# Layer 1 of a four-layer model: the choice of experts a block ahead of scan and experts' rows, in place of scan, choice and rows one block behind another

## The chip, the core and the metric

The kernel runs as one program on one core of a Trainium2 chip. The metric is device time in microseconds (us) of one execution. Most executions agree within 0.3%. The engines are named as in the profile: PE (matrix multiply; PEld is its weight load), DVE (vector), ACT (scalar), POOL (GpSimd), SP (queue of plain DMAs).

## The reference, cut to what matters

Four layers follow each other over x of shape (2, 2048, 256), that is 4096 tokens of 256 values. Each layer normalizes x and adds an attention-like branch and a feed-forward branch of the same normalized values. The change is in layer 1 alone:

```python
xn = _layernorm(x)
x = x + L1_attn(xn) + L1_ffn(xn)

def L1_attn(x):                      # the "scan" branch
    h = layernorm(x) * g + b
    xs, gate = split(h @ W_in)       # 512 + 512
    xs = silu(causal_conv4(xs) + conv_b)
    delta = mean(softplus(xs @ Wd + bd))
    y = selective_scan(xs, delta)    # 16 states, in order along each sequence
    return x + (y * silu(gate)) @ W_out

def L1_ffn(x):                       # the "choice of experts" and the "rows" branch
    sim = product keys: 8 heads x 2 halves x 128 keys
    sx, ix = top_k(sim[0], 16);  sy, iy = top_k(sim[1], 16)
    scores, index = best of all sums sx + sy           # one expert of 4096 per head
    gate = relu(scores)
    hidden = x @ W_in.T
    hidden += sum over heads of (x . in_a[index]) * gate * in_b[index]
    hidden = gelu(hidden)
    return hidden @ W_out.T + sum over heads of (hidden . out_a[index]) * gate * out_b[index]
```

As one expert per head is kept, the best pair is the best key of each half: the kernel takes two maxima and their places.

## The kernel before, in words

Everything is float32. All of x stays on the chip (`g.x`, 128 partitions x 32 tiles x 256). Layer 0 ends with results of its own experts in a DRAM table (`yd`); layer 1 gathers them into x as it starts (`fetch_experts`, lines 162 to 170: per tile of 128 tokens two indirect DMAs on POOL's queue into `yg`, each followed by a DVE multiply-add, line 169).

Layer 1 handles the tokens in 16 blocks of 256 (2 tiles of 128). Work on a block comes from three Python generators, each cut into steps by `yield`:

- `scan_block`, 9 steps. Step 1 gathers layer 0's results for the block after this one, normalizes the block (`norm2`, lines 737 to 752, into `xn`) and transposes it (`turn2`, lines 755 to 766, into `xt`). Steps 2 to 9 are the scan branch: a second normalization into `hn`, the matmuls with `W_in`, the convolution (line 674), the softplus (lines 690 to 697), the state scan (line 717), and at the end a product on POOL (line 727, `xs`), the addition of `xn` to x on POOL (line 728), the matmul with `W_out` and its addition to x on DVE (line 733). The scan of a block takes the last state and the last three columns of the block before.
- `choose_block`, 9 steps: 16 matmuls of `xt` with the prepared keys into PSUM tiles `ps_k`, for each pair a maximum (line 778) and four searches for its place (line 782), at the end the experts' numbers `ind` (line 792) and `gate`.
- `rows_block`, 18 steps and an end: for each of the two tiles `j` of a block 8 gathers of 128 rows from `tab_in` and 8 from `tab_out` (line 805, POOL's queue, tiles `G`, ten buffers), each used by DVE (lines 815, 817, 834), a GELU (line 821), matmuls into `ps_h` (lines 824, 829, 839), and the addition to x on DVE (line 842).

PSUM is divided by branch: 2 banks `ps_c` for the scan, 3 banks `ps_k` for the choice, 3 banks `ps_h` for the rows. `xn` and `xt` have three buffers, `ind` and `gate` two, most tiles of the scan one.

`weave` goes round its streams and takes from each as many steps as its weight (rows have weight 2). Round `n` of the 18 rounds weaves the scan of block `n`, the choice of block `n-1` and the rows of block `n-2`. The program's order is not the order on the engines: a scheduler of the framework orders the instructions of each engine when the program is built, by what is ready in its own account of time, with the earlier instruction in the program first. Each engine then runs its list in that order, and waits at semaphores.

Of the kernel before, what the change touches and what calls it, by code (L numbers as in the profile page):

```python
# [24 lines left out]
B, S, D = 2, 2048, 256  # L25
# [38 lines left out]
def mm(nc, out, pairs):  # L64

    n = len(pairs)
    for i, (lhsT, rhs) in enumerate(pairs):
        nc.tensor.matmul(out, lhsT, rhs, start=(i == 0), stop=(i == n - 1))  # L68
# [34 lines left out]
def wload(g, name, cols, src):  # L103
    t = g.w.tile([P, SLOT], F32, name=name, tag="w")
    g.nc.sync.dma_start(t[:, :cols], src)
    return t
# [5 lines left out]
def weave(*streams):  # L112

    live = [[n, st, 0.0] for n, st in streams]
    while live:
        for one in list(live):
            one[2] += one[0]
            while one[2] >= 1:
                one[2] -= 1
                if next(one[1], "end") == "end":  # L120
                    live.remove(one)
                    break
# [438 lines left out]
def layer1(g, tc, a, r):  # L561


    nc = g.nc
    TB = 256
    NB = T // TB
    with ExitStack() as es:
        L = Ctx()
        L.TB, L.nt, L.r = TB, TB // P, r
        wp = es.enter_context(tc.tile_pool(name="l1a", bufs=1, reuse_waits="tile"))  # L570
        g.w = es.enter_context(tc.tile_pool(name="w1", bufs=4, reuse_waits="tile"))
        psc = es.enter_context(tc.tile_pool(name="psc", bufs=2, space=bass.MemoryType.PSUM, reuse_waits="tile"))
        psk = es.enter_context(tc.tile_pool(name="psk", bufs=3, space=bass.MemoryType.PSUM, reuse_waits="tile"))
        psh = es.enter_context(tc.tile_pool(name="psh", bufs=3, space=bass.MemoryType.PSUM, reuse_waits="tile"))
        L.psc = lambda: psc.tile([P, 512], F32, name="ps_c", tag="m")
        L.psk = lambda: psk.tile([P, 512], F32, name="ps_k", tag="m")
        L.psh = lambda: psh.tile([P, 512], F32, name="ps_h", tag="m")
        L.bt = wp.tile([P, 4, 16], F32, name="bt")
        nc.sync.dma_start(L.bt, a["l1_bt"])
        L.ct = wp.tile([16, 512], F32, name="ct")  # L580
        nc.sync.dma_start(L.ct, a["l1_ct"])
        L.na = wp.tile([16, 1], F32, name="na")
        nc.sync.dma_start(L.na, a["l1_alog"])
        nc.scalar.activation(L.na, L.na, AF.Exp)
        nc.vector.tensor_scalar(L.na, L.na, -1.0, None, ALU.mult)
        L.inv = wp.tile([P, 2, 32], F32, name="inv")
        nc.vector.memset(L.inv[:, 0, :], 1.0 / 512)
        nc.vector.memset(L.inv[:, 1, :], -1.0 / 512)
        L.four = wp.tile([P, 16], F32, name="four")
        nc.vector.memset(L.four, 0.0)  # L590
        for q in range(4):
            nc.vector.memset(L.four[32 * q : 32 * q + 1, :], 1.0)
        L.wi = wload(g, "l1_wi", 2048, a["l1_wi"]).rearrange("p (k n) -> p k n", k=2)

        wk2 = wp.tile([P, 2, 2048], F32, name="wk2")
        with tc.tile_pool(name="l1q", bufs=1, reuse_waits="tile") as wq:
            wqT = wq.tile([P, 16, D], F32, name="wqT")
            for p in range(2):
                nc.sync.dma_start(wqT[:, 8 * p : 8 * p + 8, :], a["l1_wqT"][:, 8 * p : 8 * p + 8, :])
            keys = wq.tile([P, 16, P], F32, name="keys")  # L600
            nc.sync.dma_start(keys, a["l1_keys"])
            for m4 in range(4):
                for c in range(2):
                    ps = L.psk()
                    for i in range(4):
                        m = 4 * m4 + i
                        mm(nc, ps[:, i * P : (i + 1) * P], [(wqT[:, m, c * P : (c + 1) * P], keys[:, m, :])])
                    nc.scalar.copy(wk2[:, c, m4 * 512 : (m4 + 1) * 512], ps)
        L.wk2 = wk2
        L.wd = wload(g, "l1_wd", 2048, a["l1_wd"]).rearrange("p (k n) -> p k n", k=4)  # L610
        wc = wload(g, "l1_wc", 2048, a["l1_wc"])
        L.wout = wc[:, 0:1024].rearrange("p (k n) -> p k n", k=4)
        L.fwi = wc[:, 1024:2048].rearrange("p (k n) -> p k n", k=2)
        L.fwo = wload(g, "l1_fwo", 1024, a["l1_fwo"])[:, :1024].rearrange("p (k n) -> p k n", k=4)
        L.wk = es.enter_context(tc.tile_pool(name="l1b", bufs=1, reuse_waits="tile"))
        blocks = [Ctx() for _ in range(NB)]
        for n, blk in enumerate(blocks):
            blk.n, blk.tok = n, n * TB
        for n in range(NB + 2):
            streams = []  # L620
            if n < NB:
                streams.append((1, scan_block(g, L, blocks[n], blocks[n - 1] if n % (NB // B) else None)))
            if 0 <= n - 1 < NB:
                streams.append((1, choose_block(g, L, blocks[n - 1])))
            if 0 <= n - 2:
                streams.append((2, rows_block(g, a, L, blocks[n - 2])))
            weave(*streams)


def scan_block(g, L, k, prev):  # L630
# [138 lines left out]
def choose_block(g, L, k):  # L769

    nc, wk, TB, nt = g.nc, L.wk, L.TB, L.nt
    mx = wk.tile([P, 16, nt], F32, name="mx", tag="mx")
    ix = wk.tile([P, 16, nt, 8], U32, name="ix", tag="ix")
    for m4 in range(4):
        for j in range(nt):
            ps = L.psk()
            mm(nc, ps, [(k.xt[:, c, j * P : (j + 1) * P], L.wk2[:, c, m4 * 512 : (m4 + 1) * 512]) for c in range(2)])
            nc.vector.tensor_reduce(mx[:, 4 * m4 : 4 * m4 + 4, j], ps.rearrange("p (i n) -> p i n", i=4),
                                    AX.X, ALU.max)
            for i in range(4):  # L780
                m = 4 * m4 + i
                nc.vector.max_index(ix[:, m, j, :], mx[:, m, j : j + 1].to_broadcast([P, 8]),  # L782
                                    ps[:, i * P : (i + 1) * P])
            yield
    k.gate = wk.tile([P, 8, nt], F32, name="gate", tag="gate", bufs=2)
    nc.vector.tensor_tensor(k.gate, mx[:, 0:8, :], mx[:, 8:16, :], ALU.add)
    nc.vector.tensor_scalar(k.gate, k.gate, 0.0, None, ALU.max)
    fx = wk.tile([P, 16, nt], F32, name="fx", tag="fx")
    nc.vector.tensor_copy(fx, ix[:, :, :, 0])
    nc.vector.scalar_tensor_tensor(fx[:, 0:8, :], fx[:, 0:8, :], 128.0, fx[:, 8:16, :], ALU.mult, ALU.add)  # L790
    k.ind = wk.tile([P, 8, nt], U32, name="ind", tag="ind", bufs=2)
    nc.vector.tensor_scalar(k.ind, fx[:, 0:8, :], 4095.0, None, ALU.min)  # L792
    yield
# [782 lines left out]
def four_layers(ctx: ExitStack, tc: tile.TileContext, a, out):  # L1576
# [28 lines left out]
    with tc.tile_pool(name="xT0", bufs=1) as px:  # L1605
        g.xT = px.tile([P, 2, T], F32, name="xT0")
        layer0(g, tc, a, r, rt)
    layer1(g, tc, a, r)
    es.close()
    layer2(g, tc, a)  # L1610
# [98 lines left out]
```

## Time and profile before

| | us |
|---|---|
| median of 14 runs | 4264.46 (4258.58 to 4269.94) |
| the profiled execution, its own time | 4263.48 |
| span of its trace | 4261.7 |
| layer 1 in the trace: first gather of layer 0's results | 1201.2 |
| layer 1 in the trace: last addition to x (line 842) starts | 2249.4 |

Mean granted clock of PE over the span: 0.941. Over the whole span PE is busy 91%, DVE 59%, ACT 46%, POOL 31%.

The table is read so: layer 1 takes about 1049 of the 4262 us; what lies before 1201 and behind 2250 belongs to the other layers. Busy times of the profile are unions of the recorded instructions. Matmul ends are modelled, and some records are missing (a line can show fewer instances than the program has).

### The profile page before, as it was taken

The page shows a single profiled execution, that of the slowest core. Times are in us where ns is not written, and L with a number is a line of the kernel's source. Part 1 is how long each engine was busy: PE and PEld are TensorE (multiplying, and loading weights), DVE is VectorE, ACT ScalarE, POOL GpSimd, SP SyncE. Part 2 cuts the span into 40 slices and gives each one's busy share as a digit, 9 for nine tenths or more (in the row PEclk, how much of TensorE's full clock was granted, in tenths as well). Part 3 has the DMA queues.
Part 4 walks back from the last instruction along what each step waited for, and adds up shares of the span by engine and source line. Part 5 has one row for each costly group of instructions (what it writes and reads, how often), then busy time and mean ns, then how long its engine had stood idle before and what let it go on. Part 6 is the DMA issues. An engine that isn't in the chain of part 4 may idle for free.

```text
span 4261.7 us, 58911 instructions
## 1 busy us (share of the span) xinstructions
PE 3876.8 (91%) x21516; PEld 2316.6 (54%) x21516; DVE 2513.7 (59%) x6436; ACT 1975.6 (46%) x3819; POOL 1304.5 (31%) x1306
## 2 busy tenths in 40 slices
PE   6488988999978999999967999999999999999998
PEld 5366666766745556656635776776434333334332
DVE  6354444544458999999985233325765656566560
ACT  3144343434344555565523223233555555555556
POOL 1502222222256766656662112113001111111201
PEclk8687999999989999999988999999999999999999
DMA  4200122222236676777781000000000000000000
GB/s 180 95 33 33 65 73 83 71 81 81 100 116 184 197 215 198 213 207 219 215 260 39 1 1 1 1 1 26 7 6 10 8 2 19 15 6 10 4 1 26
DMA packets 110804, 330.24 MB, mean 77 GB/s; under 512 B 30610, under 2 KB 63011, under 8 KB 104115
## 3 DMA queue, kind: packets, MB, share of 16 engines
q0 software_dynamic: 52720, 264.15, 20.0%
q1 hardware_dynamic: 55330, 59.41, 4.3%
q8 instruction: 170, 2.79, 0.3%
q10 hardware_dynamic: 2464, 2.91, 0.2%
q14 instruction: 120, 0.98, 0.1%
HBM read 286.56 MB, written 33.03 MB: 75 GB/s over the span
## 4 chain that ended last, share of the span: by engine, by line
PE 53%; DVE 8%; DMA 3%; issue 2%; POOL 2%; ACT 1%; SPq 0%; DVEq 0%; ACTq 0%; POOLq 0%
PE ps_e L1345 12%; PE ps_v L1408 7%; PE ps_a L68 6%; PE ps_f L68 6%; PE ps_c L68 4%; PE ps_m L68 4%; PE ps_k L68 3%; DMA G<-in_tab_in,ind 2%; PE ps_m L1350 2%; PE ps_h L839 1%; DVE hid L817 1%; PE ps_o L1043 1%; PE ps_m L1359 1%; PE ps_s L1345 1%; DVE scr L834 1%
## 5 line engine op out<-in xcount | busy, mean ns | idle before, releaser
L1376 DVE TENSOR_REDUCE mp<-ps_m 128x1 f32<-128x512 f32 (+3 forms) x1120 | 628.5, 606 | 435.9 <-PE ps_e L1345 253.2
L1365 ACT ACTIVATE pt<-ps_e 128x512 f32<-128x512 f32 (+3 forms) x1120 | 537.2, 531 | 426.8 <-PE ps_e L1345 395.3
L1345 PE MATMUL ps_e<-qT,kT 32*128 32x512 f32 (+3 forms) x2240 | 632.2, 582 | 9.0 <-ACT pt L1365 8.8
L1350 PE MATMUL ps_m<-kT,qT 32*128 32x512 f32 (+3 forms) x2240 | 564.5, 579 | 1.1 <-DVE mp L1376 1.1
L1345 PEld LDWEIGHTS ps_e<-qT,kT 32*128 32x128 f32 x2240 | 212.6, 185 | 328.5 <-issue 122.5
L805 POOL DMA_INDIRECT G<-in_tab_in,ind x256 | 272.8, 1066 | 215.8 <-DVE ind L792 63.4
L1408 PE MATMUL ps_v<-pt,vals 128*32 128x512 f32 (+3 forms) x2560 | 307.0, 544 | 1.6 <-POOL pt L1369 0.9
L1369 POOL TENSOR_SCALAR_AFFINE_SELECT pt<-pt 128x256 f32<-128x256 f32 x256 | 103.8, 406 | 664.4 <-ACT pt L1365 664.1
L805 POOL DMA_INDIRECT G<-in_tab_out,ind x256 | 268.7, 1049 | 85.3 <-issue 34.9
L68 PE MATMUL ps_e<-xgT,we 128*128 128x256 f32 x936 | 240.9, 404 | 27.0 <-ACT xgT L306 17.6
L68 PE MATMUL ps_k<-wk,xt 128*128 128x512 f32 x512 | 254.3, 608 | 3.1 <-DVE ix L782 2.9
L68 PE MATMUL ps_f<-hb,l_b 128*128 128x512 f32 x1024 | 252.7, 399 | 1.4 <-DVE hb L1034 1.4
L1033 ACT ACTIVATE hb<-ps_f 128x512 fp32r<-128x512 f32 x128 | 75.5, 597 | 325.6 <-PE ps_f L68 325.6
L68 PEld LDWEIGHTS ps_e<-xgT,we 128*128 128x128 f32 x936 | 177.2, 198 | 70.3 <-ACT xgT L306 23.2
L68 PEld LDWEIGHTS ps_f<-hb,l_b 128*128 128x128 f32 x1024 | 189.8, 189 | 46.9 <-issue 6.7
L834 DVE CUSTOM_DVE_ANT_0 scr<-hid,G,gate 128x512 f32<-128x512 f32 x256 | 197.5, 772 | 17.5 <-DMA G<-in_tab_out,ind 12.2
L1034 DVE SCALAR_TENSOR_TENSOR hb<-ps_f,hb 128x512 fp32r<-128x512 f32 x128 | 86.9, 685 | 203.0 <-ACT hb L1033 202.7
L1350 PEld LDWEIGHTS ps_m<-kT,qT 32*128 32x128 f32 x2240 | 182.4, 185 | 26.2 <-issue 22.2
L494 DVE COPY_PREDICATED AT<-lm,ps_g 128x256 f32<-128x256 uint8 x224 | 104.8, 521 | 145.8 <-PE ps_g L489 145.7
L489 PE MATMUL ps_g<-qt,E 64*128 64x64 f32 x1792 | 139.0, 296 | 33.0 <-DVE E L485 24.2
L815 DVE CUSTOM_DVE_ANT_0 scr<-xn,G,gate 128x256 f32<-128x256 f32 x256 | 149.8, 585 | 32.4 <-DMA G<-in_tab_in,ind 31.9
L817 DVE SCALAR_TENSOR_TENSOR hid<-G,lin,hid 128x512 f32<-128x512 f32 x224 | 167.1, 746 | 2.0
(421 smaller groups left out, 7661.6 us busy)
## 6 DMA issues: line engine op xcount, KB each, us to landing
xgd<-zero SPq DMA_DIRECT2D x13, 768.0 KB, 12.5
xg<-xgd SPq DMA_DIRECT2D x39, 256.0 KB, 2.9
yd<-ye SPq DMA_DIRECT2D x39, 256.0 KB, 3.2
G<-in_tab_in,ind POOLq DMA_INDIRECT x256, 5.1
G<-in_tab_out,ind POOLq DMA_INDIRECT x256, 5.9
kT<-qk SPq DMA_DIRECT2D x256, 16.0 KB, 1.8
out<-x SPq DMA_DIRECT2D x8, 512.0 KB, 3.0
x<-in_x ACTq DMA_DIRECT2D x4, 512.0 KB, 9.3
```

Source lines behind the costliest of these rows:

```text
L68: nc.tensor.matmul(out, lhsT, rhs, start=(i == 0), stop=(i == n - 1))
L489: nc.tensor.matmul(two[r][:, n * 64 : (n + 1) * 64], E[r * 64 : (r + 1) * 64, n * P : (n + 1) * P], qt[r * 64 : (r + 1) * 64, n * 64 : (n ...
L494: nc.vector.copy_predicated(AT[:, r].rearrange("p e (n t m) -> p e n t m", t=2, m=m)[:, :, :, 1, :], lm[:, li * 64 : (li + 1) * 64].unsque ...
L805: nc.gpsimd.indirect_dma_start(G, None, a[tab], bass.IndirectOffsetOnAxis(ap=k.ind[:, h, j : j + 1], axis=0))
L815: nc.vector.tensor_tensor_reduce(scr[:, 0:D], k.xn[:, j, :], G[:, 0:D], k.gate[:, h, j : j + 1], 0.0, ALU.mult, ALU.add, lin[:, h : h + 1])
L817: nc.vector.scalar_tensor_tensor(hs, G[:, D:768], lin[:, h : h + 1], hid if h == 0 else hs, ALU.mult, ALU.add)
L834: nc.vector.tensor_tensor_reduce(scr, hs, G[:, 0:512], k.gate[:, h, j : j + 1], 0.0, ALU.mult, ALU.add, lout[:, h : h + 1])
L1345: nc.tensor.matmul(te[i // step][:, i % step, c0:512], ge.kT[row(j), kt * P : (kt + 1) * P], ge.qT[row(j), qb * 512 + c0 : (qb + 1) * 512] ...
L1350: nc.tensor.matmul(tm[i // step][:, i % step, 0:w], gm.qT[row(j), qi * P : (qi + 1) * P], gm.kT[row(j), ch * 512 : ch * 512 + w], start=Tr ...
L1365: nc.scalar.activation(pt[:, o : o + step, c0:512], te[i // step][:, :, c0:512], AF.Exp, scale=0.25)
L1376: nc.vector.tensor_reduce(gm.mp[:, qi, j : j + step, ch], tm[i // step][:, :, 0:w], AX.X, ALU.max, negate=True)
L1408: nc.tensor.matmul(av[row(j), c0:512], vals[:, kt, at + 17 * j : at + 17 * j + 32], pts[j][:, c0:512], start=first, stop=last)
```

## The change

All 16 scan generators are made first. Step 1 of a scan (gather, normalization, transpose) is taken out of the weaving and called by itself: for block 0 ahead of round 0, for block `n+1` at the end of round `n`. Round `n` then weaves the rest of the scan (steps 2 to 9) of block `n-1`, the choice of block `n`, and the rows of block `n-1`. There are 17 rounds instead of 18. No instruction is added or removed, no buffer is resized.

```diff
-        for n in range(NB + 2):
+        scans = [scan_block(g, L, k, blocks[k.n - 1] if k.n % (NB // B) else None) for k in blocks]
+        next(scans[0])
+        for n in range(NB + 1):
             streams = []
+            if n:
+                streams += [(1, scans[n - 1])]
             if n < NB:
-                streams.append((1, scan_block(g, L, blocks[n], blocks[n - 1] if n % (NB // B) else None)))
-            if 0 <= n - 1 < NB:
-                streams.append((1, choose_block(g, L, blocks[n - 1])))
-            if 0 <= n - 2:
-                streams.append((2, rows_block(g, a, L, blocks[n - 2])))
+                streams += [(1, choose_block(g, L, blocks[n]))]
+            if n:
+                streams.append((2, rows_block(g, a, L, blocks[n - 1])))
             weave(*streams)
+            if n + 1 < NB:
+                next(scans[n + 1])
```

## Prediction

> **What bounds the kernel now.** I read the page's slices first, then the busy time by stage, then single lines for where a block's steps stand in time, then the waits. Slices, one every 106.5 us (layer 1 lies in slices 12 to 22, counted from 1):
>
> ```profile
> PE   6488988999978999999967999999999999999998
> DVE  6354444544458999999985233325765656566560
> ```
>
> In the middle of layer 1 both engines stand at 9; at both ends one or both drop. The cuts by stage (columns: length, busy time and records of PE, PEld, DVE, ACT, POOL, then granted clock, DMA share, GB/s):
>
> ```profile
> 1201.00:1270.00 69.00, 48.53 (x181) 26.67 (x182) 50.50 (x174) 29.32 (x52) 47.25 (x45) 0.88 0.25 72
> 1270.00:1440.00 170.00, 153.91 (x631) 98.47 (x630) 144.67 (x457) 91.63 (x159) 115.37 (x106) 0.96 0.63 191
> 1440.00:2100.00 660.00, 637.51 (x2551) 396.27 (x2550) 618.20 (x2090) 381.70 (x656) 419.73 (x386) 0.97 0.70 209
> 2100.00:2160.00 60.00, 58.08 (x241) 36.43 (x240) 57.10 (x186) 31.64 (x55) 38.52 (x35) 1.00 0.71 222
> 2160.00:2250.00 90.00, 50.21 (x147) 30.91 (x145) 68.80 (x217) 18.43 (x41) 56.47 (x54) 0.81 0.91 268
> ```
>
> From 1440 to 2100 PE is busy 96.6% and DVE 93.7%: full rounds have nearly no room on either. The first 69 us and the last 90 us are filled to 70% and 56% on PE, 73% and 76% on DVE. Where the steps stand, from the lines of `ind` (end of a choice), of the scan's and of the rows' additions to x:
>
> ```profile
> L792 DVE TENSOR_SCALAR ind<-fx x16: 157/172/213, 1266.2 to 2194.7; 128x16 uint32<-128x16 f32 x16
> L733 DVE TENSOR_TENSOR x<-x,ps_c x16: 669/682/687, 1268.7 to 2160.3; 128x512 f32<-128x512 f32 x16
> L842 DVE TENSOR_TENSOR x<-x,ps_h x32: 380/417/430, 1316.8 to 2249.4; 128x256 f32<-128x256 f32 x32
> ```
>
> So 65 us pass before the first `ind` lets the first gather of rows go, and 89 us remain behind the last scan: two blocks of rows with one choice beside them. Between, a block takes (2160.3-1268.7)/15 = 59.4 us. The waits that matter, of DVE in the first 69 us, of PE in the last 90, of POOL in the full rounds (total, times, longest):
>
> ```profile
> DVE x L169 <- DMA yg<-yd,pos: 35.9, 17, 23.7
> PE ps_h L824 <- ACT hid L821: 29.7, 3, 11.4
> POOL x L728 <- ACT xn L751: 25.4, 7, 6.4
> ```
>
> At the start DVE stands behind layer 0's results; at the end PE stands behind the GELU, that is behind rows with nothing to fill the gap.
>
> **The change, part by part.** *Work.* No instruction comes or goes. The page counts 512 choice matmuls for 16 blocks, 32 a block, and the cut from 1440 to 2100 holds 350 of them by the cut of tile `ps_k`, so 10.94 blocks; PE 637.5/10.94 = 58.3 us a block, DVE 618.2/10.94 = 56.5. By tile in the same cut PE is busy 303.6 on `ps_c`, 173.2 on `ps_k`, 202.4 on `ps_h` (they overlap; scaled to 637.5): scan 26.0, choice 14.9, rows 17.4. DVE's choice is 167.3/10.94 = 15.3.
>
> *Start.* The first choice is no longer woven with the first scan, but stands ahead of it. `xt` of block 0 is there at 1214.4 (line 766); 16 matmuls are 14.9 us of PE, DVE's part 15.3: not before 1230. The gathers of layer 0's results (24 of 64 run before 1242, 37 before 1270) still mix with it. I put the first `ind` at 1242, between 1232 and today's 1266, nearer the low end because what the scan had in front is gone. Until then PE has done, at the pace between 1214 and 1268.7 (scan and choice, 40.9 us of work in 54.7: 0.75), 28 x 0.75 = 21 us: the choice and 6 of the scan.
>
> *End.* One block of rows stands behind the last full round, with its scan beside it. Rows alone go at 44 us a block (line 842 of block 14 at 2205.3, of block 15 at 2249.4), and need 55 from their `ind` (2194.7) to the end. The scan and rows of a block are 43.4 us of PE and 41.2 of DVE, so they are hidden in each other only almost: 52 us, between 45 and 60.
>
> *Middle, by PE.* Layer 1 is 16 x 58.3 = 933 us of PE; less 21 and 43.4 leaves 868.6. Before, the same stretch (1268.7 to 2160.3) did 933 - 40.9 - 44.4 = 847.7 in 891.6, a rate of 0.951 (44.4 is the last 90 us by count of records at the warm price: 23 of 32 of a choice, 124 of 128 of two rows). 868.6/0.951 = 913. End: 1201+41+913+52 = 2207, against 2249.8: 43 us less.
>
> *Middle, by DVE.* The five cuts sum to 939.3. In the first 41 us some 30 (50.5 x 41/69), last block 41.2, middle 868. At the rate of 1270 to 2160 (820.0/890 = 0.921) 942 us, end 2236, 14 less; at that of the full rounds (0.937) 926, end 2220, 30 less. DVE's low early rate comes with the waits for layer 0's rows, which stay one backlog; I take 0.937.
>
> Both engines bind, so the smaller gain counts more: **30 us less**.
>
> [...] In this trace PE is busy 96.6% of the full rounds, but PEld 396.27/660 = 60%. [...]
>
> *Step 1 moved.* Its 4 gathers (POOL), 4 multiply-adds, two statistics and small DVE steps, 1 root and 2 normalizations on ACT, 4 transposes, 2 copies keep their place between two rounds; what moves is the user. Before, `xt` was read a round later; now the choice that stands next reads it. From the root (1209.0) to the end of the copies (1214.4) the chain took 5.4 us, with 1.2 for the statistics (4 instructions of 0.41 and 0.17) and 1.0 for two choice matmuls 7.6 us. I cost it at nothing: rows and scan of the block before, 43.4 us of PE and 41.2 of DVE, lie in the same round and do not need it. Without that cover it costs up to 7.6 x 15 = 114 us. `ind` still stands a round ahead of its rows, and the three buffers of `xn` and `xt` get looser (held two rounds, not three); that touches the 25.4 us of POOL's waits for `xn`, which lie on no busy engine: nothing.
>
> *New order on x.* Line 728 (POOL, 1.27 us) and line 733 must now follow line 842 of the same block's first tile, and that of its second tile must follow 733. Behind 728 on POOL stand the gathers `G`, behind 733 two scan banks. The first tile's 842 comes some 30 us before the second's, 733 at the end of the round, so between 0 and, if POOL stands once a round for one gather's 5.1 us to landing, 15 x 5.1 = 77; ten buffers lie ahead of DVE, I take 0. POOL itself has room: 419.7/660.
>
> Sum against the profiled 4263.5: -30, so 4233.5; the median is 1.0 above it: 4234.
>
> **The rivals.** *Choice exposed (slower).* The order is fixed when the program is built; if it puts the normalization of the next block last and the choice's DVE work right behind it, DVE stands through the chain at each of 15 boundaries. At half of 7.6 us: 57 - 30 = 27 more, 4291; above 30/15 = 2.0 us a round it is slower. For it: DVE and PE have 6% and 3% of room, and PE waits in order behind transposes. Against: from 1440 to 2100 DVE waits for a normalization only once, 1.0 us, with two chains in each round. The new order on x would give the same sign. 0.21.
>
> *Backlog (no change).* With the rows starting at 1242, 40 gathers of layer 0's results are still to come, not 27; 13 more on POOL, each 0.95 and 0.30 between them, 16 us in front of rows' gathers; if the last block takes 60 too: -30+16+8 = -6, 4258. For it: from 1270 to 1440 DVE and PE reach only 85% and 91%. Against: POOL idles 55 of 170 there. 0.09.
>
> *Rate of the full rounds from the first.* `ind` at 1232 (PE work done 13.5), 0.966 throughout, 45 us at the end: 31 + 876/0.966 + 45 = 983, so 2184: 66 less, 4199. PE's row speaks for it, DVE's against. 0.15.
>
> **How the numbers follow.** Middle case 0.55, with the fast one 0.70 for faster; 0.09 for no change; 0.21 for slower. 0.2%, 8.5 us, is about what a measurement of this kernel can tell from none. The range reaches from just below the fast case, 4196, to 4282, most of the way to the slow rival at half exposure, leaving out some 0.04 below and 0.13 above.
>
> **What would show it.** Right: first `ind` near 1242, first line 842 some 25 us earlier, last 842 some 52 us behind that of block 14, spacing of line 733 still near 59.4. Wrong: spacing above 61.4 with DVE waiting for `ps_k` or POOL at line 728 (slow rival); DVE waiting for `G` or `yg` through 1242 to 1440 (backlog); or rows and scan of the last block taking 65 us or more.

## The result: 41 us slower, and the profile after

The changed kernel takes 4305.89 us (median of 6 runs, 4301.71 to 4314.03), the kernel before 4264.48 (28 runs). The ratio is 1.010, with a 95% interval of 1.009 to 1.011. The forecast was 4234, between 4196 and 4282: wrong in sign, and the range missed by 24 us. The profiled execution took 4310.16, its span 4308.4, 46.7 longer than before's; layer 1, from the first gather of layer 0's results (1202.5) to the start of the last addition of rows (2296.8), takes 1094.3 in place of 1048.2. So the loss lies within layer 1. From here on "the length of layer 1" is this number, of one profiled execution. Where start and end of layer 1 fall in other executions moves by some us with what lies before it, so lengths and medians are kept apart.

Behind its line 620 the changed file counts 4 lines more than the file before: `ind` is line 796, the scan's addition 737, rows' 846, POOL's product 731, the last DVE step ahead of it 728, the gathers `G` 809, DVE's product with `G` 819.

The slices of the page, as shown of before:

```profile
PE   6478988999878899899987999999999999999998
...
DVE  6355444454468988988985323334866656566560
```

The 9s of both engines in the middle have become a mixture of 8s and 9s. The cut of the full rounds (length, busy time of PE, PEld, DVE, ACT, POOL, clock, DMA share, GB/s):

```profile
1440.00:2100.00 660.00, 595.65 (x2332) 375.16 (x2331) 578.62 (x1926) 362.46 (x606) 400.85 (x371) 0.94 0.63 195
```

In it PE fell from 96.6% to 90%, DVE from 94% to 88%, and the clock from 0.97 to 0.94. It holds 320 choice matmuls in place of 350, so 10.0 blocks in place of 10.94: 66.0 us a block, not 60.3. Of the 5.7 us more, PE's busy time has 1.3 (59.6 a block, was 58.3, at the lower clock), its idle time 4.4. No engine is the bound now; something stands between them. The lines of `ind`, of the scan's and of rows' additions:

```profile
L796 DVE TENSOR_SCALAR ind<-fx x16: 157/166/168, 1239.9 to 2228.8; 128x16 uint32<-128x16 f32 x16
...
L737 DVE TENSOR_TENSOR x<-x,ps_c x16: 673/688/690, 1311.1 to 2296.0; 128x512 f32<-128x512 f32 x16
...
L846 DVE TENSOR_TENSOR x<-x,ps_h x32: 408/415/422, 1278.7 to 2296.8; 128x256 f32<-128x256 f32 x32
```

First `ind` at 1239.9, not 1266.2: the early start is there. Rows' additions start at 1278.7, not 1316.8. But the scans end (2296.0-1311.1)/15 = 65.7 us apart, not 59.4, and 15 x 6.3 = 94 us eat what both ends gave. The waits (total, times, longest):

```profile
DVE scr L819 <- DMA G<-in_tab_in,ind: 96.6, 78, 3.5
DVE x L169 <- DMA yg<-yd,pos: 30.9, 8, 23.7
...
POOL xs L731 <- DVE xs L728: 97.2, 13, 10.3
...
PE ps_h L828 <- ACT hid L825: 37.8, 23, 5.6
```

DVE now waits 97 us for gathered rows (32 before), POOL 97 for the scan's last DVE step (2 before), PE 38 for the GELU (32 before, but 30 of that in three waits at the layer's end; now 23 waits). Looked at in time, they lie at the boundaries of two rounds. One boundary, POOL first:

```profile
1763.59 2.69 POOL L731 TENSOR_TENSOR xs<-xs,sgt 128x1024 f32<-128x1024 f32 x1 [8.00 <-DVE xs L728]
1767.42 1.31 POOL L809 DMA_INDIRECT G<-in_tab_in,ind  x1 [1.14 <-DVE ln_mr L753]
...
1774.04 0.94 POOL L809 DMA_INDIRECT G<-in_tab_in,ind  x1 [3.54 <-PE ps_h L843]
```

The first gather with the new `ind` (1766.99) goes at once, the third 6.6 us later, when PE is done with a buffer. PE in the same stretch:

```profile
1768.46 4.88 PE L68 MATMUL ps_c<-l_wc,xs 128*128 128x256 f32 x16
1773.17 3.62 PE L843 MATMUL ps_h<-G,dg 128*128 128x256 f32 x16
1776.63 0.60 PE L765 MATMUL ps_c<-cst,xn 128*128 128x128 f32 x4
...
1778.36 1.88 PE L68 MATMUL ps_k<-wk,xt 128*128 128x512 f32 x4
```

The scan's last matmul and rows' last 16 stand ahead of the transposes of `xn`, which make `xt` for the next choice; its first matmul starts at 1778.36, 11.4 us behind `ind`. And DVE:

```profile
1766.99 0.16 DVE L796 TENSOR_SCALAR ind<-fx 128x16 uint32<-128x16 f32 x1
...
1773.45 0.69 DVE L737 TENSOR_TENSOR x<-x,ps_c 128x512 f32<-128x512 f32 x1 [1.17 <-PE ps_c L68]
...
1778.37 0.48 DVE L819 CUSTOM_DVE_ANT_0 scr<-xn,G,gate 128x256 f32<-128x256 f32 x1 [3.30 <-DMA G<-in_tab_in,ind]
...
1783.49 0.69 DVE L782 TENSOR_REDUCE mx<-ps_k 128x4 f32<-128x512 f32 x1
```

DVE waits for four products with `G` one after another (3.30, 1.94, 0.49, 0.47), and the first maximum of the next choice comes 16.5 us behind `ind`. Before, the same place looked like this:

```profile
1783.67 0.18 DVE L792 TENSOR_SCALAR ind<-fx 128x16 uint32<-128x16 f32 x1
1783.75 0.69 DVE L778 TENSOR_REDUCE mx<-ps_k 128x4 f32<-128x512 f32 x1
...
1787.98 0.41 DVE L715 TENSOR_TENSOR dl<-dl,ps_c 16x256 f32<-16x256 f32 x1 [0.93 <-PE ps_c L68]
...
1788.99 1.73 DVE L717 TENSOR_TENSOR_SCAN hs<-dA,hs,dl 16x256 f32<-16x256 f32 x1
```

There the next maximum follows `ind` at once, and the scan is in its middle: work that is ready. After, the choice, the scan and the rows all end at the boundary and all begin there, each behind something that is late: transposes for the choice, transposes and the matmul with `W_in` for the scan, gathers for the rows. The normalizations are not late. `xn` of the block that is chosen next was written a round earlier, 82 us before its transposes:

```profile
1693.27 1.07 ACT L755 ACTIVATE xn<-x,ln_mr,ln_rs 128x256 f32<-128x256 f32 x2
```

and `hn`, which the scan transposes at 1777.93, at 1712.57. What makes `xt` late is the place of the transposes on PE, behind the end of the scan that stands ahead of them in the program and whose two PSUM banks (`ps_c`) they share. No run tells the order from the banks.

### The profile page after: what moved, and what is told of

It reads as the page before. It is cut to its first block, busy times and chain, and to the rows that moved or that the text cites. A ratio compares the mean times of both kernels' runs of the same rounds, so it can differ in the third digit from the quotient of the medians.

```text
span 4308.4 us, 58974 instructions
## 1 busy us (share of the span) xinstructions
PE 3890.0 (90%) x21516; PEld 2331.5 (54%) x21516; DVE 2516.0 (58%) x6436; ACT 1997.8 (46%) x3826; POOL 1304.3 (30%) x1306
## 4 chain that ended last, share of the span: by engine, by line
PE 71%; DVE 14%; ACT 5%; DMA 5%; POOL 3%; issue 3%; SPq 0%; POOLq 0%; ACTq 0%; DVEq 0%
PE ps_e L1349 12%; PE ps_v L1412 6%; PE ps_g L68 6%; PE ps_e L68 6%; PE ps_a L68 6%; PE ps_f L68 6%; PE ps_c L68 5%; PE ps_m L68 4%; PE ps_g L489 2%; DVE hid L821 2%; DMA G<-in_tab_in,ind 2%; PE ps_k L68 2%; DVE ix L786 2%; PE ps_h L843 2%; PE ps_m L1354 2%
## 5 line engine op out<-in xcount | busy, mean ns | idle before, releaser
L809 POOL DMA_INDIRECT G<-in_tab_out,ind x256 | 284.9, 1113 | 106.4 <-DVE hid L821 51.6
L842 ACT ACTIVATE dg<-cst,lout 128x128 f32<-128x128 f32 x256 | 102.0, 401 | 217.9 <-DVE lout L838 127.8
L819 DVE CUSTOM_DVE_ANT_0 scr<-xn,G,gate 128x256 f32<-128x256 f32 x256 | 127.4, 497 | 96.7 <-DMA G<-in_tab_in,ind 96.6
L821 DVE SCALAR_TENSOR_TENSOR hid<-G,lin,hid 128x512 f32<-128x512 f32 x224 | 178.8, 798 | 1.1
```

The lines of the kernel that those rows point to most:

```text
L809: nc.gpsimd.indirect_dma_start(G, None, a[tab], bass.IndirectOffsetOnAxis(ap=k.ind[:, h, j : j + 1], axis=0))
L819: nc.vector.tensor_tensor_reduce(scr[:, 0:D], k.xn[:, j, :], G[:, 0:D], k.gate[:, h, j : j + 1], 0.0, ALU.mult, ALU.add, lin[:, h : h + 1])
L821: nc.vector.scalar_tensor_tensor(hs, G[:, D:768], lin[:, h : h + 1], hid if h == 0 else hs, ALU.mult, ALU.add)
```

## The experiments

Each ratio is to the kernel before, which ran beside each group of experiments (medians 4260.8 to 4265.7). Theories when the first four were made. **A**: step 1 is called one round too late, right in front of its user; called two rounds ahead, the loss goes. **B**: the new order on x. **C**: POOL's product comes late and holds the gathers behind it. **D**: the choice is too slow within its round.

**e1_norm_ahead**, step 1 two blocks ahead:

```diff
         next(scans[0])
+        next(scans[1])
...
-            if n + 1 < NB:
-                next(scans[n + 1])
+            if n + 2 < NB:
+                next(scans[n + 2])
```

> The changed kernel with step 1 of the scan (normalization and transpose) called two blocks ahead instead of one; nothing else. Theory A (the choice of the next block has nothing to begin with at the round's boundary, because its xt is made only then): spacing of the scans' ends back from 66.3 to about 60 us, DVE's idle time per round back from 8.1 to about 4, DVE's waits for G from tab_in from 97 to about 35 us, time about 4306 - 15 x 6 = 4216. Theory B (the new order of the additions to x), theory C (POOL stands at the scan's product on line 731, 97 us in 13 times, with the rows' gathers behind it) and theory D (the experts' numbers come too late): no change, 4306.

4268.12, ratio 1.0011 (1.0001 to 1.0021): 38 us below the change's 4306. In its trace the next choice no longer starts behind `ind`; at one boundary:

```profile
1740.40 1.12 PE L68 MATMUL ps_k<-wk,xt 128*128 128x512 f32 x2
```

```profile
1747.13 0.29 DVE L797 TENSOR_SCALAR ind<-fx 128x16 uint32<-128x16 f32 x1
```

Its first matmul is 6.7 us ahead of `ind`, and DVE's wait for `G` is 65.6 in place of 96.6. But the gain of both ends, that A's 4216 counted on, is still missing: A is right in part.

**e2_x_early**, the addition of `xn` to x on POOL in the scan's second step:

```diff
     norm2(g, wk, xn, hn, nt)
+    nc.gpsimd.tensor_tensor(xb, xb, xn, ALU.add)
...
     nc.gpsimd.tensor_tensor(xs, xs, sgt, ALU.mult)
-    nc.gpsimd.tensor_tensor(xb, xb, xn, ALU.add)
```

> The changed kernel with POOL's addition of xn to x (line 732) moved from the scan's last step to its second, ahead of the rows' additions to the same block in the program. Theory B: spacing back to about 60 us, time about 4216. Theories A, C and D: no change beyond 10 us, 4296 to 4316.

4311.61, 1.011 (1.0093 to 1.0127), the same as the change. B falls.

**e3_dve_product**, the product on DVE:

```diff
-    nc.gpsimd.tensor_tensor(xs, xs, sgt, ALU.mult)
+    nc.vector.tensor_tensor(xs, xs, sgt, ALU.mult)
```

> The changed kernel with the scan's product (line 731) on DVE instead of POOL: POOL no longer stands for it, DVE gets 16 instructions of 128x1024, some 1.1 us each. Theory C: DVE's waits for G from tab_in fall from 97 to about 35 us, spacing to about 61, time about 4306 - 80 + 17 = 4243. Theories A, B and D: POOL's wait moves on to the experts' numbers (line 796), which come 3 us behind the product's operand; time 4306 to 4323.

4292.41, 1.0069 (1.0052 to 1.0086): 14 less than the change. The product takes 1.22 us on DVE (1.205 to 1.224). POOL's wait did not go, it moved to the line behind the product (waits of POOL):

```profile
POOL G L809 <- DVE ln_mr L753: 72.5, 7, 14.6
...
POOL G L809 <- DVE ln_rs L751: 45.9, 7, 12.2
```

The gathers can't go before `ind`, which lies there. C is no cause of the most of it.

**e4_choose_faster**, weight 1.5 for the choice:

```diff
-                streams += [(1, choose_block(g, L, blocks[n]))]
+                streams += [(1.5, choose_block(g, L, blocks[n]))]
```

> The changed kernel with weight 1.5 instead of 1 for the choice of experts in the weaving: the choice ends after two thirds of a round. Theory D: the gathers of the next rows can start at the end of the rows in front, DVE's waits for G from tab_in fall from 97 to about 35 us, time about 4220. Theory A: the next choice still starts with the round and has nothing ready; the experts' numbers being early helps the boundary partly, because gathers then fill it: 4270 to 4306. Theories B and C: no change, 4306.

4351.77, 1.0205 (1.0187 to 1.0222): 46 worse than the change. D falls. A choice that is over early leaves even less to do at the round's end: at the eleven boundaries between the choices of blocks 3 and 14 the next choice's first matmul comes 22 to 25 us behind `ind` (7 to 12 in the change).

From e1's trace came theory **E**: with step 1 out of the weaving the scan has 8 steps for 9 passes, so it now runs a pass ahead of choice and rows in every round; put back by one pass, with step 1 early, the middle keeps before's pace. Against it **P**: the new pairing of the blocks is what costs.

**e7_ahead_and_pass** (e1 and one empty pass) and **e8_pass_only** (the change and one empty pass), the pass at the end of step 1:

```diff
     yield
+    yield
```

> The run with step 1 two blocks ahead, and beside it a second, empty yield behind step 1, so that the rest of the scan starts one pass later in each weaving, as it did before the change (where step 1 took the first pass). Theory E (what is left of the longer round, 63.2 us against 59.4, comes from the scan running one pass ahead of choice and rows): spacing back to about 59.4 us, time about 4268 - 15 x 3.8 = 4211, below the kernel before. Theory P (it comes from scan and rows of one block standing in one round, whose additions to x wait for each other): no change, 4268.

> The changed kernel with the empty yield alone, step 1 one block ahead as in the change. Theory E: spacing from 65.7 to about 62 us, time about 4306 - 57 = 4249. Theory A alone (the choice has nothing to begin with) or theory P: no change, 4306.

e7: 4218.60, 0.9896 (0.9879 to 0.9912), faster than before by 46 us and than the change by 87. Its cut from 1440 to 2100, its lines and its waits:

```profile
1440.00:2100.00 660.00, 632.15 (x2569) 395.50 (x2568) 638.49 (x2138) 379.11 (x657) 456.00 (x417) 0.99 0.71 217
```

```profile
L798 DVE TENSOR_SCALAR ind<-fx x16: 154/164/214, 1231.1 to 2124.5; 128x16 uint32<-128x16 f32 x16
...
L739 DVE TENSOR_TENSOR x<-x,ps_c x16: 656/674/686, 1303.5 to 2206.3; 128x512 f32<-128x512 f32 x16
```

```profile
DVE scr L821 <- DMA G<-in_tab_in,ind: 34.3, 33, 4.2
...
POOL xs L733 <- DVE xs L730: 15.1, 1, 15.1
```

Both engines are back at 96 to 97%, the scans end (2206.3-1303.5)/15 = 60.2 apart, DVE's wait for `G` is nearly what it was before (31.9). Its layer 1 is 1014.1 long (1193.1 to 2207.2), 34 less than before; the other 12 of the 46 lie outside layer 1, in work that is the same, so that 34 is the safer figure for what the order in layer 1 gave. e8: 4321.16, 1.0129 (1.0112 to 1.0146), 15 worse than the change, where E gave 4249. The pass by itself was expected to help and hurts:

| | no pass | one empty pass |
|---|---|---|
| step 1 one block ahead (the change) | 4306 | 4321 |
| step 1 two blocks ahead | 4268 | 4219 |

So E holds in one row of the table only.

**e6_norm_end_only**, the 18 rounds and the pairing of before, but step 1 called at the end of the round in front:

```diff
-        for n in range(NB + 1):
+        for n in range(NB + 2):
...
+                streams += [(1, scans[n])]
+            if 0 <= n - 1 < NB:
+                streams += [(1, choose_block(g, L, blocks[n - 1]))]
+            if 0 <= n - 2:
+                streams.append((2, rows_block(g, a, L, blocks[n - 2])))
```

> The kernel before with one part of the change: step 1 of the scan taken out of the weaving and called at the end of the round in front; 18 rounds, scan of block n, choice of n-1, rows of n-2 as before. The xt is then still there a round ahead of its choice. Theory A: no change, 4261. Theory E: the scan runs one pass ahead, spacing 63, time about 4261 + 57 = 4318. Theory P: no change, 4261.

4312.35, 1.0111 (1.0095 to 1.0128): taking step 1 out of the weaving, and nothing else, costs 48 us. Here `xt` is used by a choice a whole round later, and the choice is not exposed: at the same eleven boundaries its first matmul is 5 to 14 us ahead of `ind`. The scan, which runs a pass ahead of choice and rows, is what is left. That is by elimination: no run put the empty pass into this form.

**e5_scan_with_choose**, scan and choice of block n together, rows of n-1:

```diff
-            if n:
-                streams += [(1, scans[n - 1])]
             if n < NB:
+                streams += [(1, scans[n])]
                 streams += [(1, choose_block(g, L, blocks[n]))]
```

> The changed kernel with the rest of the scan of block n, not n-1, in round n: scan and choice of one block together, rows a block behind; step 1 at the end of the round in front as in the change, 17 rounds. Theory A: the choice still waits for its xt at the boundary, and now the scan too, spacing 66 us or more; the last block has no scan beside its rows, time 4300 to 4330. Theory P: additions to x no longer meet in one round, spacing about 62, time about 4250. Theory E: as theory A says, since the scan is one pass ahead here too.

4311.18, 1.0097 (1.008 to 1.0115): another pairing, the same loss. P falls with e5 and e6.

What does the pass do? **E1**: choice and rows stand ahead of the scan's beginning. **E2**: the scan's end comes later. And **F**: ten buffers for `G` are too few for the new pairing.

**e9_pass_at_end** (e1, the pass ahead of the scan's last step), **e10_two_passes** (e1, two passes behind step 1), **e11_scan_last** (e1, no pass, the scan named last in each round's list):

```diff
@@ e9
     yield
+    yield
     nc.gpsimd.tensor_tensor(xs, xs, sgt, ALU.mult)
@@ e10
     yield
+    yield
+    yield
@@ e11
-            if n:
-                streams += [(1, scans[n - 1])]
...
                 streams.append((2, rows_block(g, a, L, blocks[n - 1])))
+                streams += [(1, scans[n - 1])]
```

> Step 1 two blocks ahead as in the first run, and the empty pass not behind step 1 but ahead of the scan's last step (product, matmul with W_out, additions to x). Theory E1 (what counts is that choice and rows of the round stand ahead of the scan's beginning): no change against step 1 ahead alone, 4268. Theory E2 (what counts is that the scan's end stands a pass later against choice and rows): time near 4219, as with the empty pass in front.

> Step 1 two blocks ahead and two empty passes behind it instead of one. Theory E1: the second pass moves nothing that counts, 4215 to 4225. Theory E2: the scan's end now lies behind the choice's and against the rows' end, either way: the spacing leaves 60 us by over 1 us and the time 4219 by over 15.

> Step 1 two blocks ahead, no empty pass, but in each pass of the weaving the scan comes last, behind choice and rows, instead of first. Theory E1: choice and rows stand ahead of the scan's beginning, as with the empty pass: about 4219. Theory E2: the scan's end moves by less than a pass: 4235 to 4268.

e9: 4262.01, 0.9991 (0.9981 to 1.0), 6 less than e1. e11: 4226.63, 0.9915 (0.9898 to 0.9931), most of the step from e1 to e7 by order within a pass alone (its layer 1 is 1010.6 long, e7's 1014.1). e10: 4237.67, 0.9935 (0.9919 to 0.9952): a second pass costs 19 again. What the edits moved on PE, as the start of the scan's matmuls behind `ind`, median of ten boundaries (blocks 4 to 13):

| | first with `W_in` | first with `W_out` | time |
|---|---|---|---|
| before | 22.5 | 15.0 | 4264 |
| e6 | 15.6 | 6.3 | 4312 |
| e1 | 16.1 | 6.6 | 4268 |
| e9 | 16.1 | 7.2 | 4262 |
| e7 | 20.8 | 13.7 | 4219 |
| e11 | 20.8 | 13.7 | 4227 |
| e10 | 27.8 | 15.3 | 4238 |

So E is seen on the engine: in e6 and e1, without the pass, the scan stands 6 to 9 us earlier than before. But e9, which was to test E2, left the scan's end nearly where e1 had it, and e7 and e11 moved beginning and end together; E1 and E2 are not told apart. e10 moved mostly the beginning, and lost. Of the places tried e7's is the best, and both sides of it lose.

**e12_more_G**, the change with twelve buffers:

```diff
-NG = 10
+NG = 12
```

> The changed kernel with 12 instead of 10 buffers for the gathered rows. Theory F (DVE starves on G because the buffers come free too late behind the matmuls of line 843): POOL's waits for these matmuls, 5.6 us a round, and DVE's for G, 5.9 a round, fall by half, time about 4306 - 45 = 4261. Theories A and E (nothing else is ready at the boundary): gathers come up to 2.5 us earlier, time 4290 to 4306.

4309.01, 1.0112 (1.0095 to 1.0129). F falls: the wait for `G` stays, though POOL's wait for PE to free these buffers (line 843) went from 76.0 to 24.8, more than the half that F asked for.

```profile
DVE scr L819 <- DMA G<-in_tab_in,ind: 85.8, 92, 2.9
```

Two points were left: why e3 gained 14, and whether pass and early step 1 need each other in any form. Theory **L** for the first, from the change's trace, where the step of line 791 took 2.31 us beside POOL's product and 0.17 elsewhere: a DVE instruction stands while a tensor-tensor of POOL runs.

**e13_both_on_dve** (e7 with product and addition of `xn` on DVE) and **e14_after_on_dve** (the change with both on DVE):

```diff
-    nc.gpsimd.tensor_tensor(xs, xs, sgt, ALU.mult)
-    nc.gpsimd.tensor_tensor(xb, xb, xn, ALU.add)
+    nc.vector.tensor_tensor(xs, xs, sgt, ALU.mult)
+    nc.vector.tensor_tensor(xb, xb, xn, ALU.add)
```

> The two early steps of the fastest version (normalization two blocks ahead, one empty pass), and the product xs and the addition of xn to x go from POOL to DVE. Lock theory L: while a POOL tensor-tensor runs, a DVE instruction stands still (in that version's trace 55 us of DVE time above the usual length lie on instructions that overlap these two POOL instructions). Without them DVE saves 55 and pays 16 x (1.22 + 0.69) = 31: 24 us less, 4195 of 4219, or down to 4211 if PE (96% busy) sets the pace. Rival: the long records are only ends that were drawn late, DVE gets 31 us more: 4235 to 4250. Theory C, that POOL's late start at the product is what costs: it waited there 15 us once in that version, so 4204 to 4219, and no stretched instruction need vanish.

> The changed kernel with the product and the addition of xn on DVE. L: its trace has 49 us of stretched DVE instructions; less 31 of new work: 19 less at most, 4287 to 4295, so near the 4292 of the product alone; and since before has as many stretched (47), L is no cause of the change's loss. C: the loss comes back by most of 41: 4265 to 4275. Rival (DVE pays 31): 4320 to 4337.

e14: 4289.01, 1.0067 (1.0049 to 1.0085), 17 less than the change, where L gave 11 to 19 and C gave 31 to 41. e13: 4210.84, 0.9884 (0.9866 to 0.9901), at the upper end of L's 4195 to 4211; this is the fastest version, though its interval overlaps e7's. Its layer 1 is 993.0 long, 21 less than e7's; PE is busy 637.98 of the 660 us there, so PE may take part of what DVE gains. The medians differ by 8 only, since e7's profiled execution is 12 to 14 shorter outside layer 1 than those of before, e11 and e13. In e14's trace the step of line 791 lasts 0.171 us at most.

**e15_last_only**, the change with the scan named last, step 1 one block ahead (e11 without its early step 1):

```diff
-            if n:
-                streams += [(1, scans[n - 1])]
...
                 streams.append((2, rows_block(g, a, L, blocks[n - 1])))
+                streams += [(1, scans[n - 1])]
```

> The changed kernel with the scan as the last stream of each pass, normalization one block ahead as in the change. If the two parts work only together (as the empty pass did): not under 4300, 4300 to 4325. If the order within a pass acts by itself and the empty pass failed for another reason: 41 less as with the early normalization, 4260 to 4270.

4320.64, 1.0143 (1.0121 to 1.0165): the same as e8. In both forms the later scan gains some 41 to 50 with step 1 early, and loses 15 without. That much is shown, and e8's trace shows why the two hang together. `ind` at one boundary, and PE behind it:

```profile
1764.96 0.17 DVE L797 TENSOR_SCALAR ind<-fx 128x16 uint32<-128x16 f32 x1
```

```profile
1780.70 3.72 PE L68 MATMUL ps_c<-l_wc,xs 128*128 128x256 f32 x16 [1.05 <-POOL xs L732]
...
1786.44 0.44 PE L766 MATMUL ps_c<-cst,xn 128*128 128x128 f32 x2 [0.52 <-DVE x L738]
1786.72 1.88 PE L68 MATMUL ps_k<-wk,xt 128*128 128x512 f32 x4
```

The later scan's last matmul starts 15.7 us behind `ind` (in the change 1.5), the transposes of `xn` come behind it and even wait for the scan's addition to x, and the next choice starts 21.8 us behind `ind` (11.4). At the eleven boundaries the next choice starts 18 to 23 us behind `ind` in e8 and 18 to 22 in e15, against 7 to 12 in the change. With step 1 one block ahead, whatever puts off the scan puts off the next choice; with step 1 two blocks ahead these transposes serve a choice a round later. How 15 us in all follow from 10 a boundary is not worked out; e8's DVE waits 111.6 us for `G`, against 96.6 in the change.

## Why the prediction was wrong, point by point

**Start**: `ind` at 1242 (1232 to 1266) was forecast, 1239.9 measured. Right. **End**: 52 us (45 to 60) from block 14's last addition to block 15's; 2239.5 to 2296.8 are 57. Within its bounds. In e7 the last block takes 62 (2145.2 to 2207.2), 2 above them.

**Middle**: from the first `ind` to block 14's last addition 926 us were forecast by DVE's pace, 913 by PE's; measured were 2239.5-1239.9 = 1000. With the chosen sum (the end at 2220) the error splits into -2 at the start, +74 in the middle and +5 at the end: 77. It is all in one term.

**The step that failed** is *Step 1 moved*: "I cost it at nothing: rows and scan of the block before, 43.4 us of PE and 41.2 of DVE, lie in the same round and do not need it." The cover was counted in amount, not in place. There are 43 us of other work in the round, but little of it is ready at the boundary: rows wait for gathers that go out with the same `ind`, the scan for its own transposes, and the transposes for `xt` stand behind the end of the scan in front. At the boundary shown the next choice starts 11.4 us behind `ind`, before it started 4 us ahead of it. e1 shows that part by itself: 38 us. The working's price without cover, 7.6 us a round, is that of another chain, most of it a normalization, and the normalization was never exposed; that the middle lost 74/15 = 4.9 a round, not far from it, is chance.

**What was not priced at all** is that a step taken out of a weave shifts everything behind it. The scan went from 9 woven steps to 8, one pass ahead of choice and rows, and it is named before them in each pass as well. "What moves is the user" was true of step 1, and steps 2 to 9 moved too. It is worth 49 us between e1 and e7 (42 by e11), and e6, which has nothing else of the change, lost 48. The two parts don't add up: without the first, mending the second loses.

**The rate** 0.951 and 0.937 was carried over from before as if it belonged to the work. It belongs to the order: from 1440 to 2100 PE and DVE were busy 0.97 and 0.94 of the time before, 0.90 and 0.88 after, 0.96 and 0.97 in e7, with the same instructions.

**The sum of the edges** comes out, as a sum. 30 us less was the choice, 43 by PE; with the pace of the middle restored, layer 1 is 34 shorter in e7 and 38 in e11 (1201.7 to 2212.3). By parts e7 has 38 from the first gather to the first `ind` (41 forecast), 914 to block 14's last addition (926, by PE 913) and 62 for the last block (52), so the errors of the parts cancel for the most. By DVE the prediction had 14 to 30 less; e7 and e11 lie between that and PE's 43. e13 took some of DVE's load away, and layer 1 got 21 shorter again in the profile (8 by the medians): this fits DVE as a bound beside PE, as the row of busy times had said.

**The new order on x** at 0: right (e2). **Backlog**: not seen, DVE's wait for `yg` over layer 1 fell from 42.1 to 30.9. **Rate of the full rounds**, 66 less: only e13's layer 1, 55 less, comes near. **Choice exposed**, the rival with 0.21, was the nearest: its sign and its place at the boundary were right, what it would show in the profile half. The spacing above 61.4 came, but not DVE waiting for `ps_k` nor POOL at the addition of `xn`. DVE stood at products with `G` because the choice's maxima had been listed behind them: at the boundary shown the first four choice matmuls end by 1780.24, DVE stands for `G` another 0.9, 0.49 and 0.47 us, and its first maximum comes at 1783.49. What was held against it, that "DVE waits for a normalization only once", was read from a trace in which the user of `xt` came a round later, and so could say nothing on this; and what the change exposed is the transposes, not the normalization that the rival named.

## What to carry to other kernels

When a step is moved out of an interleaved schedule, write down for each boundary what is ready on each engine in the 10 us behind it; cover counts only where it can start. Count the steps of the stream that is left: if it has one less, everything behind moves a pass ahead, and an empty step can give the old phase back; it did so here only with the moved step's result early. Ask also what stands ahead of the moved step on its engine. The wait that an engine is seen in (here for the gathers) need not be the cause: two more buffers in e12 did nothing, and giving the engine other ready work in e7 removed two thirds of it.

## What the runs showed of the hardware

**The clock fell where PE had only short gaps.** At the boundary of the change shown above PE has no gap over 1.5 us; from 1758 to 1765 it has gaps of 1.5, 0.2 and 0.7 and, between them, matmuls over 16 partitions (16*128). Ends of matmuls are modelled, so the gaps may be somewhat longer. The granted clock in the cut of that boundary (columns as above):

```profile
1758.00:1763.00 5.00, 3.26 (x9) 1.82 (x8) 3.84 (x17) 4.93 (x8) 0.00 (x0) 0.78 0.08 31
1763.00:1768.00 5.00, 4.23 (x11) 3.21 (x12) 5.00 (x14) 1.41 (x5) 3.27 (x2) 0.50 0.00 0
1768.00:1774.00 6.00, 6.00 (x22) 4.97 (x21) 4.76 (x14) 0.51 (x2) 2.20 (x2) 0.75 0.47 131
1774.00:1779.00 5.00, 5.00 (x25) 3.82 (x25) 1.66 (x8) 3.11 (x9) 3.77 (x4) 1.00 0.52 151
```

It stands at 0.50 and is back at 1.00 within 11 us. The matmul with `W_out` starts at 1768.46, before that: its first five instructions there last 0.63 us each, its last ten 0.38. All 16 keep PE busy for 3.6 to 3.7 us in 15 rounds of before (5.4 in one) and for 3.6 to 5.3 in the change, 71.6 us over the layer in place of 60.6. So the boundary seems to cost twice, by PE's 2.4 us of gaps and by the slower matmuls behind them. What lowers the clock, no run shows.

**A DVE step lasted until POOL's product beside it ended.** The step that sets negative gates to 0 (line 791, 128x16) takes 0.16 to 0.18 us in 11 of the change's 16 rounds; in the other five it started 0.4 us behind the start of POOL's product and took 2.31, to 0.03 behind the product's end. Its durations (min, median, max in ns) in the change and in e14:

```profile
L791 DVE TENSOR_SCALAR gate<-gate x16: 163/166/2314, 1238.8 to 2225.8; 128x16 f32<-128x16 f32 x16
```

```profile
L791 DVE TENSOR_SCALAR gate<-gate x16: 155/169/171, 1234.7 to 2206.9; 128x16 f32<-128x16 f32 x16
```

Summed over layer 1, what DVE instructions last above the median of their kind beside POOL's two tensor-tensors is 45 us before, 49 in the change, 55 in e7, of POOL's 58 to 60; e13 and e14 have both on DVE. It is no cause of the change's loss, as it was there before, but DVE's "busy" time held it all along. Why a step lasts so long there, no run shows.
